# A mixture-of-experts kernel with six single tiles ahead of its paired units in place of seven, and its table of rows made in two single tiles

## The chip, the cores and the metric

The kernel runs on one core of a Trainium2 chip. Its time is the device time of one execution in microseconds (us); a profiled execution has in addition a span, from its first to its last instruction. TensorE (PE) multiplies matrices and transposes through a product with an identity; it writes to PSUM, of which the kernel holds eight banks PB[0] to PB[7]. VectorE (DVE) and ScalarE (ACT) read PSUM and do everything elementwise. GpSimd (POOL) issues the indirect transfers, which gather and scatter rows by a list of row numbers. SyncE (SP) issues the plain transfers. All engines run their own programs in order and wait for each other by semaphores.

## The reference

4096 tokens (64 x 64) of 256 values; every token goes to two of eight experts. An expert is a three-layer network 256 -> 512 -> 512 -> 256.

```python
var = jnp.mean(x * x, axis=-1, keepdims=True)
xn = rms_w * (x * jax.lax.rsqrt(var + EPS))
gate = xn @ wg_W + wg_b + (genre_embed @ gg_W + gg_b)
gate_w = jax.nn.softmax(gate, axis=-1)
topk_w, topk_i = jax.lax.top_k(gate_w, TOP_K)          # TOP_K = 2
cw = jnp.sum(jax.nn.one_hot(topk_i, E, dtype=x.dtype) * topk_w[..., None], axis=-2)
h1 = jax.nn.relu(jnp.einsum('bsh,ehm->bsem', x, W1) + b1)
h2 = jax.nn.relu(jnp.einsum('bsem,emn->bsen', h1, W2) + b2)
out_e = jnp.einsum('bsen,enh->bseh', h2, W3) + b3
out = x + jnp.einsum('bseh,bse->bsh', out_e, cw)
```

The reference computes every expert for every token and weights the result with `cw`, which is zero for six of the eight. The kernel computes only the two that count.

## The kernel before

The 8192 pairs of a token and an expert are put into tiles of 128 pairs of one expert. The routing is found in two parts: part A (`pA`) holds the first eight tokens of each partition, part B (`pB`) the other 24.

**Single tiles.** The first `F` = 7 tiles are one each of experts 0 to 6, filled with the first 128 pairs of that expert in part A. Their row numbers (`idxA`) are known early, so TensorE can work on them while the rest of the routing is computed. A single tile is gathered into `xg`, transposed (`transpose_x`), and goes through `layer1`, `layer2` and `layer3`: 8, 16 and 4 products, each of which the trace shows as two instructions. `head_step(u)` writes the program of single tile u: layer 1 of u, the transposes of tile u+1, layer 3 of u−1, layer 2 of u. The last single tile is done by `step`.

**The table of rows.** All pairs that are left are numbered by expert and tile; `idxR` is the list of their rows, one column per tile. It is made by products: for each of 64 pairs per partition (2 choices x 32 tokens) VectorE makes a one-hot of the place within a tile (`ohl`, from `lo16`) and one of the tile's number (`ohh`, a compare of `whole`, a row of tile numbers, with `hi16`), multiplies the latter with the token's number (`ohv`), and TensorE adds up 64 products in PB[7] (`table`, L646). VectorE does this in four chunks of 16 pairs (`rest`, L779 to L790), `idxR` follows from the sum in four operations (L794 to L797), and POOL gathers the rows of the first two units (`gather_unit`). `rest` is a generator, and `until(label)` writes its program up to a label; so `head_step` sets which piece stands where in the engines' programs.

**Units.** What is left is done in units of one expert: four tiles (512 columns), then one last unit for each expert, 9 to 16 strips of 32 columns wide, then pairs of tiles (256 columns). `SHAPES` lists combinations of (units of four, pairs, widths of the last units in falling order); the kernel has one program of the tail for each, and the first shape into which the counts fit is taken. A unit is wider than a tile and done by `step_fast` with the seven products of Strassen's method in Winograd's form (`Fast`): layer 1 of the unit is `f`, layer 2 is `g`; `f.p(k)` are its products, `f.mix(k)` differences of the inputs by VectorE, `f.fold` sums of weight blocks by VectorE, `f.c11` and so on the sums that form the blocks of the result, `f.r1`, `f.r22`, `f.r21` the relus by ScalarE. For the first unit (u == F) `transpose_x` turns its four gathered tiles (`xgE`) through TensorE into PB[4] and PB[7]; VectorE copies one half of the features into `xT` and ScalarE the other (L943). The rows of later units are turned through a scratch array and VectorE's transposes.

**Weights of the pairs.** `pB.weights` and `pB.spread` form each token's weight for each expert, three elementwise operations on POOL (L452 to L454), and write them to `cwdR`, from which `gather_cw` reads them by row.

The order in the program is written by hand; nothing is moved by a scheduler.

Of the kernel before, what the change touches and what calls it, by code (L numbers as in the profile page):

```python
# [12 lines left out]
F16 = mybir.dt.float16  # L13
# [8 lines left out]
SHAPES = [  # L22
# [26 lines left out]
]  # L49
# [3 lines left out]
def kernel(  # L53
# [17 lines left out]
    nc = tc.nc  # L71
# [18 lines left out]
    NPAIR = NT * TOPK  # L90
    F = E - 1

# [228 lines left out]
    class Part:  # L321
# [127 lines left out]

        def spread(self, cwd, cw8, i0):  # L450
            by_token = [self.ohe[:, k].rearrange("p e i -> p i e") for k in range(TOPK)]
            nc.gpsimd.tensor_tensor(self.cw8, by_token[0], self.over_e(self.t["den"]), ALU.mult)  # L452
            nc.gpsimd.tensor_tensor(self.w, by_token[1], self.over_e(self.t["d2"]), ALU.mult)
            nc.gpsimd.tensor_tensor(self.cw8, self.cw8, self.w, ALU.add)  # L454
            nc.gpsimd.dma_start(cwd.rearrange("(p i) e -> p i e", p=P)[:, i0 : i0 + cw8.shape[1], :], cw8)

# [182 lines left out]

    mms, placed = [], []  # L640

# [6 lines left out]
    def rest():  # L648
# [121 lines left out]
        LW, HW = P * GC // 2, NREST * GC // 2  # L770
        ohh = bigf[:, 0:HW].bitcast(F16).rearrange("p (g t) -> p g t", g=GC)

        def cols(c):
            return slice(c * GC, (c + 1) * GC)

        def low_of(c):
# [4 lines left out]

        ohls = [low_of(0)]
        for c in range(NCH):
            b0 = HW + (c % 3) * (LW + HW) + LW
            ohv = bigf[:, b0 : b0 + HW].bitcast(F16).rearrange("p (g t) -> p g t", g=GC)
            if c:
                ohls.append(low_of(c))
            V.tensor_tensor(ohh, whole, hi16[:, cols(c)].unsqueeze(2).to_broadcast([P, GC, NREST]), ALU.is_equal)
            i0 = c * GC % NI
            V.tensor_tensor(ohv, ohh, tokw[:, i0 : i0 + GC], ALU.mult)  # L790
# [3 lines left out]
        V.tensor_scalar(sa, tab, 0.0, -1.0, ALU.is_gt, ALU.mult)  # L794
        V.tensor_scalar(sb, tab, 0.0, float(NT), ALU.is_equal, ALU.mult)
# [129 lines left out]
    def transpose_x(u):  # L925
        bs, w, s0 = tiles(u), len(tiles(u)), slots(u).start
        if u > F:
            for k in range(w):
                V.transpose(  # L929
                    xT[:, :, s0 + k, :].rearrange("p c (b k) -> p k c b", b=SQ),  # L930
                    shs[:, s0 + k].rearrange("p k (a c) -> p k c a", a=SQ),
                )
            return
        if u < F:
            tps = [PB[4][:, c * BT : (c + 1) * BT] for c in range(HC)]
        else:
            tps = [PB[4], PB[7]]
        for c in range(HC):
            for k, b in enumerate(bs):
                g = ring(run, [P, H], "xg", 3, b) if u < F else xgR[(u - F) % 2][:, k]  # L940
                nc.tensor.transpose(tps[c][:, ts(k, BT)], g.rearrange("p (r c) -> p c r", c=HC)[:, c], ident)
            if u == F:
                (nc.scalar.copy if c else V.tensor_copy)(  # L943
                    xT[:, c, slots(u), :], tps[c].rearrange("p (s t) -> p s t", s=w)
                )
        if u < F:
            nc.scalar.copy(xT[:, :, s0, :], PB[4][:, 0 : HC * BT].rearrange("p (c t) -> p c t", c=HC))

# [125 lines left out]
    class Fast:  # L1074
# [108 lines left out]
        def c22(self):  # L1183
            V.tensor_tensor(self.dst(1, 1), self.tall(self.U), self.q[2], ALU.add)  # L1184

        def relu(self, n, out, src):
            nc.scalar.activation(out, src, AF.Relu, bias=ww[self.u][1][:, self.l, n : n + 1])  # L1187
# [194 lines left out]
    behind_fills = []  # L1382
    NF = 4

    def head_step(u):
# [3 lines left out]
        for k in range(3 * u, min(3 * u + 3, F)):  # L1389
            gather_cw(k)  # L1390
        layer1(u)
        if u == 0:
# [15 lines left out]
        if u > 1:  # L1408
            scaled(u - 1, "A")
        if u == F - 2:  # L1410
            until("chunk1")
            table(2 * GC)
        if u == 2:
            layer3_of(u - 1, range(HB))
            ranks_of_rest()
            layer3_of(u - 1, range(HB, MC))
            until("kinds")
        else:
            layer3(u - 1)
        if u - 1 + RING < F:  # L1420
# [3 lines left out]
        if u in (2, 4):  # L1424
            nc.sync.dma_start(b3_sb[:, u + 2 : u + 4], b3[u + 2 : u + 4].unsqueeze(0).to_broadcast([P, 2, H]))
        if u == F - 2:
            until("chunk2")
            table(3 * GC)
            until("chunk3")
            layer2(u, {2: table})  # L1430
            until("fetched")
            stream_3(F, mybir.EngineType.SP)
            fill(1)
            stream_1(F + 1, mybir.EngineType.SP)
            stow(F + 1)
            shuffle(F + 1)
            give(u - 2)
            give(u - 1, held=held)
            until("spread")
            return  # L1440
        if u == 2:
            layer2(u, {0: pB.exps})
        elif u == 3:
            until("places")
            layer2(u, {1: spread_map})
        else:
            layer2(u)
        if u == 1:
            scaled(0, "A")
        if u != F - 3:  # L1450
            give(u - 1)
        if u == 1:
            until("counts")
        if u == F - 3:
            until("chunk0")
            stream_1(F, mybir.EngineType.SP)
            fill(0)

    def fill(k):
# [13 lines left out]
    def step(u, last):  # L1473
# [5 lines left out]
        if u < last:  # L1479
            layer1(u)  # L1480
            if u >= F:
                streams(u, last)
            stage_2(u)
# [38 lines left out]
    def step_fast(u, last):  # L1522

        if u == F:
            transpose_x(u)
        far = fetches_of(u, last)
# [12 lines left out]
        if u == F:  # L1539
            scaled(u - 1, "A")  # L1540
            layer3_of(u - 1, range(HB))
            f.p(1)
            f.mix(1)
            f.p(5)
            f.mix(2)
            f.mix(3)
            f.p(2)
            f.c11()
            f.mix(4)
            f.p(6)  # L1550
            f.p(3)
            f.c12()
# [3 lines left out]
            f.r22()  # L1556
            layer3_of(u - 1, range(HB, MC))
            f.p(4)
            f.r21()
            g.mix(1)  # L1560
# [161 lines left out]
    with tc.manual_schedule():  # L1722
# [5 lines left out]
        gather(2)  # L1728
        pA.spread(cwdA, pA.cw8, 0)
        other = rest()  # L1730

# [61 lines left out]
```

## Time and profile before

| | |
|---|---|
| median of 3 runs | 448.32 us (448.28 to 450.24) |
| profiled execution | 448.61 us, span 446.9 us |
| PE, DVE, ACT, POOL busy | 98%, 83%, 54%, 63% of the span |
| seven single tiles and the table | up to 75.60 us |
| first unit's transposes to the second product of its layer 2 | 75.60 to 88.71 us |
| five units of four tiles, eight last units, six pairs | from there on |

The times in the timelines count from the span's start. An instruction's duration overlaps with the next one's on TensorE, so what a piece of TensorE's program costs is read from the distance between starts. In brackets stands how long an engine was idle before an instruction and what ended the wait. "L646" is line 646 of the kernel; a line may be that of a helper.

### The profile page before, as it was taken

How to read it: one execution, taken by the hardware profiler on the slowest of the kernel's cores; microseconds unless marked ns; L12 is line 12 of the kernel's file. 1: busy time of each engine (PE TensorE's matmuls, PEld its weight loads, DVE VectorE, ACT ScalarE, POOL GpSimd, SP SyncE). 2: the span in 40 equal slices, each digit the busy share in tenths (PEclk: the TensorE clock that was granted, in tenths of full speed). 3: DMA queues.
4: the chain of work that ended last, by engine and by line, in shares of the span. 5: the costliest groups of instructions: out<-in, count | busy, mean ns of one | idle time of the engine just before them, and what ended most of it. 6: DMA issues, size and time to landing. Idle time of an engine off the chain costs nothing. (4 is left out here: it accounts for less than half of the span.)

```text
span 446.9 us, 9223 instructions
## 1 busy us (share of the span) xinstructions
PE 438.7 (98%) x2941; PEld 408.6 (91%) x2941; DVE 369.5 (83%) x967; ACT 242.2 (54%) x572; POOL 279.8 (63%) x237
## 2 busy tenths in 40 slices
PE   9999998999999999999999999999999999999995
PEld 8699997889898999989899999999999889999994
DVE  6898957697979888897979797988877879889962
ACT  5855533547382746555564737474454465655561
POOL 7846316778788877575858483848857447764323
PEclk9999999999999999999999999999999999999999
DMA  8999999579568575455547363736756545766312
GB/s 310 331 352 393 369 364 354 142 229 216 175 126 200 118 162 150 120 120 150 120 126 150 85 150 70 172 92 145 164 149 137 143 117 130 186 169 168 72 15 50
DMA packets 75983, 78.11 MB, mean 175 GB/s; under 512 B 35471, under 2 KB 64114, under 8 KB 75796
## 3 DMA queue, kind: packets, MB, share of 16 engines
q1 hardware_dynamic: 49376, 42.51, 30.0%
q0 software_dynamic: 14912, 17.60, 22.8%
q10 hardware_dynamic: 11636, 17.32, 11.9%
q8 instruction: 25, 0.41, 0.4%
q14 instruction: 34, 0.28, 0.2%
HBM read 61.81 MB, written 20.25 MB: 184 GB/s over the span
## 5 line engine op out<-in xcount | busy, mean ns | idle before, releaser
L1349 POOL DMA_INDIRECT out_dram<-ys,idxR x60 | 97.9, 1632 | 88.6 <-DVE ys L1335 46.8
L1166 PE MATMUL pb<-hid,big 128*128 128x256 f32 (+7 forms) x456 | 84.6, 329 | 0.0
L1187 ACT ACTIVATE hid<-hid,bb 128x256 f32<-128x256 f32 (+12 forms) x152 | 73.1, 530 | 15.5 <-DVE hid L1184 6.3
L874 POOL DMA_INDIRECT cg<-cwdR,idxR x60 | 67.4, 1123 | 19.9 <-issue 17.7
L1166 PEld LDWEIGHTS pb<-hid,big 128*128 128x128 f32 x456 | 72.1, 191 | 4.9 <-issue 0.8
L1175 ACT COPY q1s<-pb 128x512 f32<-128x512 f32 (+7 forms) x57 | 27.5, 482 | 62.1 <-PE pb L1166 61.2
L1166 PE MATMUL pb<-mixB,big 128*128 128x256 f32 (+7 forms) x304 | 56.3, 328 | 0.0
L1175 ACT COPY big<-pb 128x512 f32<-128x512 f32 (+7 forms) x57 | 27.5, 482 | 52.1 <-PE pb L1166 52.1
L1166 PE MATMUL pb<-hotA,big 128*128 128x256 f32 (+7 forms) x304 | 53.2, 328 | 0.0
L1288 PE MATMUL pb<-w3r,hid 128*128 128x256 f32 (+1 forms) x216 | 51.2, 381 | 0.0
L1166 PEld LDWEIGHTS pb<-mixB,big 128*128 128x128 f32 x304 | 48.5, 191 | 2.8
L1166 PEld LDWEIGHTS pb<-hotA,big 128*128 128x128 f32 x304 | 47.9, 191 | 2.9
L1166 PE MATMUL pb<-mixX,iotx 128*128 128x256 f32 (+7 forms) x228 | 46.9, 328 | 0.0
L874 POOL DMA_INDIRECT xgE<-in_x_dram,idxR x32 | 35.8, 1119 | 17.6 <-DVE ib L802 8.2
L1288 PEld LDWEIGHTS pb<-w3r,hid 128*128 128x128 f32 (+1 forms) x216 | 39.1, 190 | 5.2 <-issue 0.8
L1166 PEld LDWEIGHTS pb<-mixX,iotx 128*128 128x128 f32 x228 | 37.4, 191 | 2.5 <-ACT q1s L1175 0.2
L874 POOL DMA_INDIRECT big<-in_x_dram,idxR x28 | 32.2, 1149 | 8.5 <-issue 7.9
L1187 ACT ACTIVATE hid<-pb,bb 128x256 f32<-128x256 f32 (+7 forms) x76 | 27.8, 417 | 15.3 <-PE pb L1166 12.6
L1166 PE MATMUL pb<-xT,w1r 128*128 128x256 f32 (+7 forms) x152 | 31.2, 328 | 0.0
L929 DVE STREAM_TRANSPOSE xT<-gTs 128x256 f32<-128x256 f32 x56 | 29.5, 632 | 0.0
L1067 PE MATMUL pb<-hid,w2a 128*128 128x128 f32 x224 | 27.1, 276 | 0.0
L1067 PEld LDWEIGHTS pb<-hid,w2a 128*128 128x128 f32 x224 | 26.4, 192 | 0.3
(342 smaller groups left out, 841.8 us busy)
## 6 DMA issues: line engine op xcount, KB each, us to landing
w3r<-in_L_cond_W_dram ACTq DMA_DIRECT2D x17, 512.0 KB, 4.7
w2a<-in_L_cond_W_dram SPq DMA_DIRECT2D x8, 1024.0 KB, 13.7
w1r<-in_L_cond_W_dram ACTq DMA_DIRECT2D x16, 512.0 KB
w1r<-in_L_cond_W_dram SPq DMA_DIRECT2D x10, 512.0 KB, 9.5
w3r<-in_L_cond_W_dram SPq DMA_DIRECT2D x9, 512.0 KB, 12.3
big<-in_x_dram SPq DMA_DIRECT2D x8, 512.0 KB, 5.4
gTs<-scr SPq DMA_DIRECT2D x8, 512.0 KB, 4.5
out_dram<-in_x_dram SPq DMA_DIRECT2D x4, 768.0 KB
```

Of the source, the lines that this page charges most:

```text
L874: return nc.gpsimd.indirect_dma_start(out=dst, out_offset=None, in_=src, in_offset=bass.IndirectOffsetOnAxis(ap=index(b), axis=0), bounds_ ...
L929: V.transpose(xT[:, :, s0 + k, :].rearrange("p c (b k) -> p k c b", b=SQ), shs[:, s0 + k].rearrange("p k (a c) -> p k c a", a=SQ),)
L1067: nc.tensor.matmul(ph, lhsT=w2[:, m, ts(n, P)], rhs=hid[0][:, m, 0:BT], start=(m == 0), stop=(m == MC - 1))
L1166: nc.tensor.matmul(bank[:, ts(n, self.w)], lhsT=w[:, c, ts(n, P)], rhs=x[:, c], start=new and n == 0 and c == 0, stop=n == HB - 1 and c == ...
L1175: nc.scalar.copy(self.q[(1, 6, 5).index(k)], self.tall(self.X if k == 5 else self.U))
L1187: nc.scalar.activation(out, src, AF.Relu, bias=ww[self.u][1][:, self.l, n : n + 1])
L1288: nc.tensor.matmul(sums(u, k)[0 : cols.stop - cols.start], lhsT=hid[1][:, n, cols], rhs=w3[:, n, :], start=(i == 0), stop=(i == MC - 1))
L1349: add = nc.gpsimd.indirect_dma_start(out=orows, out_offset=bass.IndirectOffsetOnAxis(ap=index(b)[0:n], axis=0), in_=y[0:n], in_offset=None ...
```

## The change

- `F` is 6: there is no single tile of expert 6; its rows go into the units. `idxR` has 71 columns, not 70, and `SHAPES` is a new list of 26.
- For chunks 1 to 3 ScalarE writes `hi16` out to the full size (`spread_high`), and VectorE's compare reads that in place of a spread-out operand. Two places (`homes`) hold it in turn.
- Chunks 0 and 1 and the first 32 table products now stand in `head_step(4)`, chunks 2 and 3, the weights, the other 32 products and `idxR` in `step(5)` (`rows_of_rest`), behind layer 1 of the last single tile.
- `pB.weights` and `pB.spread` stand ahead of the table's last operations; `spread` runs on VectorE, its write to `cwdR` on SP's queue.
- For the first unit the tiles are turned by twos: two tiles, copied, then `f.p(1)`, the third tile, `f.p(2)`, the fourth, copied. The order of products and differences is new. `p4_apart` puts product 4 into a bank of its own; ScalarE copies it and VectorE adds it (`c21`), and `r2` is the relu.

```diff
 SHAPES = [
-    (5, 6, (16, 15, 15, 14, 12, 11, 10, 9)),
...
+    (5, 6, (16, 16, 15, 15, 14, 11, 10, 9)),
...
-    F = E - 1
+    F = E - 2
...
-        ohls = [low_of(0)]
+        spread_high.append(lambda c: nc.scalar.copy(high_at(c), across(c)))
+        yield "spreads"
+        ohls = []
         for c in range(NCH):
...
-            V.tensor_tensor(ohh, whole, hi16[:, cols(c)].unsqueeze(2).to_broadcast([P, GC, NREST]), ALU.is_equal)
+            V.tensor_tensor(ohh, whole, ohh if c else across(c), ALU.is_equal)
...
+        pB.weights()
+        pB.spread(cwdR, cw8B, 0, V, nc.sync)
+        yield "spread"
         V.tensor_scalar(sa, tab, 0.0, -1.0, ALU.is_gt, ALU.mult)
...
-        pB.weights()
-        nc.gpsimd.tensor_copy(cw8B[:, 0:NA, :], pA.cw8)
-        pB.spread(cwdR, cw8B, 0)
-        yield "spread"
...
+        def p4_apart(self, bank):
+            a22, out = self.blocks()[2], bank[:, 0 : HB * self.w]
+            for n in range(HB):
+                for c in range(self.k):
+                    nc.tensor.matmul(
+                        out[:, ts(n, self.w)],
+                        lhsT=a22[:, c, ts(n, P)],
+                        rhs=self.t[3][:, c],
+                        start=n == 0 and c == 0,
+                        stop=n == HB - 1 and c == self.k - 1,
+                        skip_group_check=True,
+                    )
+            nc.scalar.copy(self.q[0], self.tall(out))
+        def c21(self):
+            V.tensor_tensor(self.dst(1, 0), self.tall(self.U), self.q[0], ALU.add)
...
+        elif u == 4:
+            until("chunk0")
+            table(GC)
+            spread_high[0](2)
+            until("chunk1")
+            layer2(u, {0: lambda: spread_high[0](3), 2: lambda: table(2 * GC)})
...
+    def rows_of_rest():
+        until("chunk3")
+        until("spread")
+        table()
+        until("fetched")
...
         if u == F:
-            transpose_x(u)
+            f = Fast(u, 0)
+            turn_tile(u, 0)
+            turn_tile(u, 1)
+            turned_two(u, 0)
+            scaled(u - 1, "A")
+            layer3_of(u - 1, range(HB))
+            f.p(1)
+            turn_tile(u, 2)
+            f.p(2)
+            f.c11()
+            turn_tile(u, 3)
+            turned_two(u, 2)
+            f.mix(1)
+            f.mix(2)
...
-            layer3_of(u - 1, range(HB, MC))
-            f.p(4)
-            f.r21()
+            f.p4_apart(PB[3])
+            f.c21()
+            f.r2()
             g.mix(1)
```

What this moves, at the two places of which the prediction speaks. A row is the line, the operation, what it writes and reads, and its size. First VectorE, at the end of the chunks (`big` holds the one-hots, `pb_75` is the bank of the table). Before:

```order
L788 TENSOR_TENSOR big<-whole,hi_575 128x1120
L790 TENSOR_TENSOR big<-big,xgE 128x1120
L794 TENSOR_SCALAR sa<-pb_75 128x70
L795 TENSOR_SCALAR sb<-pb_75 128x70
L796 SCALAR_TENSOR_TENSOR sa<-pb_75,sa 128x70
L797 TENSOR_TENSOR idxR<-sa,sb 128x70
```

After:

```order
L800 TENSOR_TENSOR big<-whole,big 128x1136
L802 TENSOR_TENSOR big<-big,xgE 128x1136
L446 TENSOR_REDUCE denB<-wB 128x24
L447 RECIPROCAL denB<-denB 128x24
L448 TENSOR_TENSOR d2B<-d2B,denB 128x24
L452 TENSOR_TENSOR cw8B<-ohB,denB 128x192
L453 TENSOR_TENSOR wB<-ohB,d2B 128x192
L454 TENSOR_TENSOR cw8B<-cw8B,wB 128x192
L809 TENSOR_SCALAR sa<-pb_75 128x71
```

The last compare reads `big`, where ScalarE has written, in place of `hi`; the weights and the three column operations stand between the last one-hot and the table's first operation.

Second TensorE, from the last product of layer 2 of the last single tile into the first unit (`pb0` to `pb7` are the banks, `xgE` the gathered rows, `hid1` with `w3r` is layer 3 of the single tile). Before:

```order
L1067 MATMUL pb3_71<-hid0_90,w2a_85 128x128 x4
L941 MATMUL pb4_72<-ident_92,xgE_186 128x128 x4
L941 MATMUL pb7_75<-ident_92,xgE_186 128x128 x4
L1295 MATMUL pb5_73<-w3r0_86,hid1_91 128x256 x2
L1166 MATMUL pb0_68<-xT_188,w1r1_83 128x256 x2
L1166 MATMUL pb1_69<-mixX_193,iotx_112 128x256 x2
```

After:

```order
L1080 MATMUL pb3_71<-hid0_90,w2a_85 128x128 x4
L953 MATMUL pb4_72<-ident_92,xgE_186 128x128
L953 MATMUL pb7_75<-ident_92,xgE_186 128x128
...
L1330 MATMUL pb6_74<-w3r2_88,hid1_91 128x256 x2
L1179 MATMUL pb0_68<-xT_188,w1r0_82 128x256 x2
...
L1179 MATMUL pb2_70<-xT_188,w1r0_82 128x256 x2
...
L1330 MATMUL pb6_74<-w3r2_88,hid1_91 128x256 x2
L1179 MATMUL pb1_69<-mixX_193,iotx_112 128x256 x2
```

Where eight transposes stood in a row ahead of everything, two tiles are turned ahead of the first half of layer 3 and `f.p(1)` (into `pb0`), one ahead of `f.p(2)` (into `pb2`) and one behind it; `f.p(5)` (into `pb1`), which needs a difference of the inputs, comes behind the second half of layer 3.

More of the change, by code (lines that the diff above doesn't have):

```diff
@@ L448, in weights, with spread @@
             V.tensor_tensor(d2, d2, den, ALU.mult)
-        def spread(self, cwd, cw8, i0):
+        def spread(self, cwd, cw8, i0, eng=nc.gpsimd, queue=nc.gpsimd):
             by_token = [self.ohe[:, k].rearrange("p e i -> p i e") for k in range(TOPK)]
[L452 to L455, printed above, removed]
+            eng.tensor_tensor(self.cw8, by_token[0], self.over_e(self.t["den"]), ALU.mult)
+            eng.tensor_tensor(self.w, by_token[1], self.over_e(self.t["d2"]), ALU.mult)
+            eng.tensor_tensor(self.cw8, self.cw8, self.w, ALU.add)
+            queue.dma_start(cwd.rearrange("(p i) e -> p i e", p=P)[:, i0 : i0 + cw8.shape[1], :], cw8)
     pA, pB = Part("A", 0, NA), Part("B", NA, NI)
@@ L638, in last_upright @@
         pB.norm(False)
-    mms, placed = [], []
+    mms, placed, spread_high = [], [], []
     def table(n=TOPK * NI):
@@ L770, in rest, with high_at, across @@
         LW, HW = P * GC // 2, NREST * GC // 2
-        ohh = bigf[:, 0:HW].bitcast(F16).rearrange("p (g t) -> p g t", g=GC)
+        homes = (0, HW + 3 * (LW + HW))
+        assert homes[1] + HW <= NG * TPB * H - GA * TPB * H
         def cols(c):
             return slice(c * GC, (c + 1) * GC)
+        def high_at(c):
+            h0 = homes[c % 2]
+            return bigf[:, h0 : h0 + HW].bitcast(F16).rearrange("p (g t) -> p g t", g=GC)
+        def across(c):
+            return hi16[:, cols(c)].unsqueeze(2).to_broadcast([P, GC, NREST])
         def low_of(c):
@@ L785, in rest @@
             ohv = bigf[:, b0 : b0 + HW].bitcast(F16).rearrange("p (g t) -> p g t", g=GC)
-            if c:
-                ohls.append(low_of(c))
-            V.tensor_tensor(ohh, whole, hi16[:, cols(c)].unsqueeze(2).to_broadcast([P, GC, NREST]), ALU.is_equal)
+            while len(ohls) <= min(c + (c > 0), NCH - 1):
+                ohls.append(low_of(len(ohls)))
+            ohh = high_at(c)
+            V.tensor_tensor(ohh, whole, ohh if c else across(c), ALU.is_equal)
             i0 = c * GC % NI
@@ L933, in transpose_x, with turn_tile, turned_two @@
             return
[L934 to L937, printed above, removed]
         for c in range(HC):
[L939 to L947, printed above, removed]
+            g = ring(run, [P, H], "xg", 3, u)
+            nc.tensor.transpose(PB[4][:, ts(c, BT)], g.rearrange("p (r c) -> p c r", c=HC)[:, c], ident)
+        nc.scalar.copy(xT[:, :, s0, :], PB[4][:, 0 : HC * BT].rearrange("p (c t) -> p c t", c=HC))
+    def turn_tile(u, k):
+        g = xgR[(u - F) % 2][:, k]
+        for c, bank in enumerate((PB[4], PB[7])):
+            nc.tensor.transpose(bank[:, ts(k, BT)], g.rearrange("p (r c) -> p c r", c=HC)[:, c], ident)
+    def turned_two(u, k0):
+        tps = [PB[4], PB[7]]
+        for c in range(HC):
+            (nc.scalar.copy if c else V.tensor_copy)(
+                xT[:, c, k0 : k0 + 2, :], tps[c][:, k0 * BT : (k0 + 2) * BT].rearrange("p (s t) -> p s t", s=2)
+            )
     def arena(t, sizes):
@@ L1184, in c22, with r2 @@
             V.tensor_tensor(self.dst(1, 1), self.tall(self.U), self.q[2], ALU.add)
+        def p4_apart(self, bank):
[9 more added lines that the diff above has]
+                        skip_group_check=True,
+                    )
+            nc.scalar.copy(self.q[0], self.tall(out))
+        def c21(self):
+            V.tensor_tensor(self.dst(1, 0), self.tall(self.U), self.q[0], ALU.add)
+        def r2(self):
+            for n in range(HB):
+                x = self.dst(1, 0)[:, n]
+                self.relu(HB + n, x, x)
         def relu(self, n, out, src):
@@ L1383 @@
     NF = 4
+    KNOWN = 5
     def head_step(u):
@@ L1391, in head_step @@
         layer1(u)
+        if u == 4:
+            spread_high[0](1)
         if u == 0:
@@ L1409, in head_step @@
             scaled(u - 1, "A")
-        if u == F - 2:
-            until("chunk1")
-            table(2 * GC)
         if u == 2:
-            layer3_of(u - 1, range(HB))
             ranks_of_rest()
-            layer3_of(u - 1, range(HB, MC))
             until("kinds")
-        else:
-            layer3(u - 1)
+        if u == KNOWN:
+            rows_of_rest()
+        layer3(u - 1)
         if u - 1 + RING < F:
@@ L1425, in head_step @@
             nc.sync.dma_start(b3_sb[:, u + 2 : u + 4], b3[u + 2 : u + 4].unsqueeze(0).to_broadcast([P, 2, H]))
[L1426 to L1440, printed above, removed]
         if u == 2:
@@ L1449, in head_step @@
             scaled(0, "A")
-        if u != F - 3:
+        if u < F - 3:
             give(u - 1)
@@ L1454, in head_step @@
         if u == F - 3:
-            until("chunk0")
             stream_1(F, mybir.EngineType.SP)
             fill(0)
+        if u == F - 2:
+            stream_3(F, mybir.EngineType.SP)
+            fill(1)
+            stream_1(F + 1, mybir.EngineType.SP)
+            give(u - 2)
+            give(u - 1, held=held)
+            if u == KNOWN:
+                stow(F + 1)
+                shuffle(F + 1)
+    def rows_of_rest():
[3 more added lines that the diff above has]
+        until("fetched")
     def fill(k):
@@ L1480, in step @@
             layer1(u)
+            if u == KNOWN:
+                rows_of_rest()
+                stow(F + 1)
+                shuffle(F + 1)
             if u >= F:
@@ L1539, in step_fast @@
         if u == F:
[L1540 to L1543, printed above, removed]
+            layer3_of(u - 1, range(HB, MC))
             f.p(5)
[L1545 to L1548, printed above, removed]
             f.mix(4)
             f.p(6)
+            f.mix(3)
             f.p(3)
@@ L1729 @@
         pA.spread(cwdA, pA.cw8, 0)
+        nc.gpsimd.tensor_copy(cw8B[:, 0:NA, :], pA.cw8)
         other = rest()
```

2 lines of the change are left out of this document (1 added, 1 removed), and 50 rows, old and new, of the table SHAPES.

## The prediction

> **What bounds the kernel.** I read the page first: the span, and how much of it each engine is busy.
> ```profile
> span 446.9 us, 9223 instructions
> PE 438.7 (98%) x2941; PEld 408.6 (91%) x2941; DVE 369.5 (83%) x967; ACT 242.2 (54%) x572; POOL 279.8 (63%) x237
> ```
> TensorE works 98% of the span, so an edit is worth what it takes from or adds to TensorE's program, plus what it does to the few waits. The list of waits for TensorE (engine, what it waited for, us in total, times, longest) names the largest:
> ```profile
> PE pb L941 <- DMA xgE<-in_x_dram,idxR: 1.6, 3, 0.9
> ```
> It is the first four-tile unit waiting for its gathered rows of x. The timeline of TensorE (start, us, line, output and inputs, count, and in brackets the idle time before) shows the stretch around it, and one ordinary single tile ahead of it:
> ```profile
> 49.74 1.95 PE L1057 MATMUL pb<-xT,w1r 128*128 128x128 f32 x16
> ...
> 51.76 1.89 PE L1288 MATMUL pb<-w3r,hid 128*128 128x256 f32 x8
> 53.49 3.73 PE L1067 MATMUL pb<-hid,w2a 128*128 128x128 f32 x32
> 57.06 1.95 PE L1057 MATMUL pb<-xT,w1r 128*128 128x128 f32 x16
> ...
> 59.08 2.12 PE L646 MATMUL pb<-big 128*128 128x70 f16 x32
> 61.04 1.97 PE L1288 MATMUL pb<-w3r,hid 128*128 128x256 f32 x8
> ...
> 72.03 3.73 PE L1067 MATMUL pb<-hid,w2a 128*128 128x128 f32 x32
> 75.60 0.28 PE L941 MATMUL pb<-ident,xgE 128*128 128x128 f32 x1
> 76.36 0.39 PE L941 MATMUL pb<-ident,xgE 128*128 128x128 f32 x1 [0.48 <-DMA xgE<-in_x_dram,idxR]
> ...
> 78.95 1.03 PE L1295 MATMUL pb<-w3r,hid 128*128 128x256 f32 x4
> 79.81 1.03 PE L1166 MATMUL pb<-xT,w1r 128*128 128x256 f32 x4
> ...
> 88.71 3.62 PE L1166 MATMUL pb<-hotA,big 128*128 128x256 f32 x16
> ```
> Ends are modelled, so I take distances between starts. A single tile costs 57.06 − 49.74 = 7.32 us. Layer 3 of one tile is 53.49 − 51.76 = 1.73, half the table of rows (32 products) is 61.04 − 59.08 = 1.96, layer 2 of a single tile 75.60 − 72.03 = 3.57. The unit after the single tiles begins its own products (p1) at 79.81, and at 88.71 TensorE issues the second product of its layer 2; from there no wait of note is left. I follow the change to that same product.
>
> **Part 1: one single tile fewer, −7.32 us of TensorE.** Its 128 rows don't vanish. Counting the two largest gates of every token of the reference's inputs, the expert that loses its single tile goes from 639 to 767 remaining rows, 20 to 24 strips of 32. The last unit of that expert widens from 12 to 16 strips, and the first shape of the new list fits. The starts of consecutive full units, and the products of the 12-strip unit (192 columns to a product):
> ```profile
> 168.77 1.03 PE L1166 MATMUL pb<-xT,w1r 128*128 128x256 f32 x4
> 193.15 1.03 PE L1166 MATMUL pb<-xT,w1r 128*128 128x256 f32 x4
> ...
> 301.99 2.76 PE L1166 MATMUL pb<-hotA,big 128*128 128x192 f32 x16
> 304.59 1.46 PE L1166 MATMUL pb<-hid,big 128*128 128x192 f32 x8
> ```
> A full unit costs 193.15 − 168.77 = 24.38 us. The 12-strip unit has 84 product instructions at 2.60 / 16 = 0.1625 us, 13.65, and three tiles of layer 3 at 1.73, 5.19: 18.84. **So the tail grows by 24.38 − 18.84 = 5.54 us**, and TensorE's whole work shrinks by only 1.78.
>
> **Part 2: when the rows of the first unit are known.** After the change the table's 64 products stand in the last two single tiles. TensorE, from the unchanged 49.74: 7.32 + 1.96 for tile 4 with half of the products, about 1.79 for layer 1 of tile 5 (51.76 − 49.74 = 2.02 holds two transposes besides), 1.96 for the other half ends at 62.77; layer 3 and layer 2, 1.73 + 3.57, end at 68.07. Before, the same point is 75.60: 7.53 sooner. VectorE must have the one-hots ready by 60.81. Its groups (mean ns of one before the bar's end) and its timeline:
> ```profile
> L788 DVE TENSOR_TENSOR big<-whole,hi 128x1120 f16<-128x1120 f16 x4 | 5.3, 1320 | 0.0
> L790 DVE TENSOR_TENSOR big<-big,xgE 128x1120 f16<-128x1120 f16 x4 | 3.0, 742 | 0.1
> L404 DVE TENSOR_TENSOR ohB<-gTs 128x192 f32<-128x192 f32 x2 | 1.2, 624 | 0.1
> L452 POOL TENSOR_TENSOR cw8B<-ohB,denB 128x192 f32<-128x192 f32 x1 | 1.2, 1243 | 0.0
> ```
> ```profile
> 60.25 1.23 DVE L779 TENSOR_TENSOR big<-iotx,lo 128x2048 f16<-128x2048 f16 x1 [1.39 <-PE pb L646]
> ...
> 62.75 0.74 DVE L790 TENSOR_TENSOR big<-big,xgE 128x1120 f16<-128x1120 f16 x1
> 67.74 0.23 DVE L794 TENSOR_SCALAR sa<-pb 128x70 f32<-128x70 f32 x1 [4.25 <-PE pb L646]
> ...
> 68.28 0.23 DVE L797 TENSOR_TENSOR idxR<-sa,sb 128x70 int32<-128x70 f32 x1
> ...
> 69.00 0.87 DVE L1335 SCALAR_TENSOR_TENSOR ys<-pb,cg,bc 128x256 f32<-128x256 f32 x2
> ...
> 70.60 0.35 DVE L1031 TENSOR_SCALAR bc<-b_sb,cg 128x256 f32<-128x256 f32 x1
> ...
> 76.49 0.68 DVE L1124 TENSOR_TENSOR big<-big 128x512 f32<-128x512 f32 x1
> ```
> The one-hots end at 63.49 with 1.39 of waiting inside. Three compares whose operand ScalarE has written out read packed data like L790; no row shows that compare, so it costs 0.74 to 1.32, and I take 0.74, the same size and type with no spread operand: 3 × 0.58 = 1.74 less. That gives 63.49 − 1.39 − 1.74 = 60.4, in time. (The two `give` steps of 0.4 that now stand between the chunks are about made up by the one taken from ahead of them and by the ranks, which now stand ahead of layer 3 of tile 1.) ScalarE's three copies are about 1.3 each, an estimate from the 0.59 that its 512 columns take at 80.88 below; they fall where it is half idle (54% on the page), and without that cover they would hold up their compares one for one. Then come the weight columns: the reductions, 70.60 − 69.00 − 0.80 = 0.8, and three operations that POOL did. They are bounded by L404 (0.62, strided as they are) and POOL's own 1.24; I take 0.62: the end is 60.4 + 0.8 + 1.9 = 63.1, against 64.9 at the upper bound. TensorE's last product ends at 62.77 and shows to VectorE at about 63.0. So TensorE and VectorE arrive together, and I put the first table operation at 63.1. POOL's timeline, and at the end a gather and the SP copy that waited for it:
> ```profile
> 68.78 1.04 POOL L874 DMA_INDIRECT xgE<-in_x_dram,idxR  x1 [8.18 <-DVE ib L802]
> 70.13 1.01 POOL L874 DMA_INDIRECT xgE<-in_x_dram,idxR  x1 [0.30 <-issue]
> ...
> 98.65 1.00 POOL L874 DMA_INDIRECT xgE<-in_x_dram,idxR  x1 [0.30 <-PE pb L1166]
> ```
> ```profile
> 101.45 0.38 SPq L913 DMA_DIRECT2D scr<-xgE  x1
> ```
> The first gather starts 68.78 − 67.74 = 1.04 after the first table operation, so at 64.1, **4.7 us sooner, while TensorE asks 7.53 sooner**. The second tile's gather starts 1.35 later and lands 76.36 − 70.13 = 6.23 after its start: 71.7. The gather at 98.65 landed within 2.8. What differs is the load on the DMA engines, by the windows (busy us of the engines, granted clock, and last the DMA share and GB/s):
> ```profile
> 57.06:75.60 18.54, 18.54 (x181) 18.08 (x179) 12.13 (x29) 6.55 (x18) 7.20 (x6) 1.00 1.05 389
> ```
> Weights and the filling of the output keep them full up to the first unit. The change drops two weight loads (1 MB, 2.6 us at 389 GB/s), so where they ran dry at about 76 they now do at 73 or later, and the rows of 64 to 72 still meet the load: I keep 6.23.
>
> [...] Here the loaded gather took 6.23 from start to landing and the unloaded one 2.8, so the trace sides with the load. [...]
>
> **Part 3: turning by twos.** TensorE is ready at 68.07, turns the first two tiles by 72.1, and does half of layer 3 (0.86) during the copy (about 0.42): p1 at 73.0. Before it was 79.81, so 6.8 sooner. From p1 to the product of 88.71 it took 8.90 before. After: seven products of 0.865, 6.05; half of layer 3, 0.86; two turns, 0.5; the first layer-2 product, 1.73: 9.14. Two new waits come on top. The second product waits for VectorE, which first does c11 (0.69), then the copy (0.42), then the first difference (0.43): about 0.4 uncovered. And the first difference of layer 2 now stands behind c21, which waits for ScalarE's copy of p4, queued behind four relus; by the durations of these (0.69, 0.59 and 2.13):
> ```profile
> 80.88 0.59 ACT L1175 COPY q1s<-pb 128x512 f32<-128x512 f32 x1 [0.74 <-PE pb L1166]
> ...
> 85.13 2.13 ACT L1187 ACTIVATE hid<-hid,bb 128x512 f32<-128x512 f32 x4 [1.07 <-DVE hid L1181]
> ```
> ```profile
> 79.39 0.43 DVE L1149 TENSOR_TENSOR mixX<-xT 128x256 f32<-128x256 f32 x1
> ...
> 82.67 0.69 DVE L1178 TENSOR_TENSOR hid<-pb,q1s 128x512 f32<-128x512 f32 x1 [1.99 <-PE pb L1166]
> ```
> the relus end 2.1 after c12, copy, c21 and difference follow, 0.59 + 0.69 + 0.69, while TensorE from p3's end has 1.73 of p7 and p4 and 1.73 of its first layer-2 product: 0.7 (c12) + 2.1 + 2.0 − 3.5, about 1.3 uncovered. The product of 88.71 comes at 73.0 + 9.14 + 1.7 = 83.8, **4.9 us sooner**.
>
> POOL loses the three column operations and the cwdR write. SP issues that write now; behind it in SP stand the loads for the second unit, which wait for that unit's gathers anyway, and the weights are read a unit later. The second unit's rows come 4.7 sooner too, against the 4.9 by which TensorE asks for them sooner. I cost these at nothing; if the 0.2 is exposed, that is their price.
>
> **The sum.** −4.9 + 5.54 = +0.6. The profiled execution took 448.61 (span 446.9, 1.7 around it): 449.2. The median of the runs is 0.3 lower, so **449.0 us**.
>
> **Rivals.**
> Early rows: if the rows land like the one at 98.65, the wait goes; but VectorE's sums of weight blocks end at 77.17, 8.89 after idxR began, less 1.6 for what has moved ahead (69.00 to 70.60), so at 70.9, and only then does it copy: p1 at 71.4, 1.6 sooner, **447.4**. For it: 1 MB less; against: the full window.
> VectorE last (slower): if the compare stays at 1.32 and the three column operations cost POOL's 1.24, VectorE ends at 60.4 + 1.74 + 0.8 + 3.7 = 66.6. It decides from 63.0 on: rows 3.5 later, **452.5**; with one of the two, 450.8. For it: no row shows either operation; against: L790 and L404.
> Cold TensorE (slower): the timeline's first rows show it.
> ```profile
> 0.86 3.75 PE L318 MATMUL pb<-const-float32-1.0 128*128 128x128 f32 x16 [0.86 <-PEq L1779]
> ```
> There 16 products took as long as the 32 at 72.03: half speed. If the new wait, 68.07 to 72.1 with only transposes in it, brings that back for 3.5 us, 1.75 is lost: **450.8**. Against: before, 75.60 to 78.95 held only transposes as well, and 78.95 to 79.81 ran four products at full speed. [...]
> The change not doing what it says: another shape taken in the tail. The counts speak against it.
>
> **Chances.** Forecast 0.62, early rows 0.15, VectorE last 0.13, cold 0.06, other 0.04. Half a per cent, 2.2 us, is about what a measurement can tell from no change: 446.1 to 450.6. Faster than that 0.06 (early rows and the sum of part 3 too dear by 1.3), slower 0.17, same 0.77. The range takes in early rows below and one late VectorE operation above: 446.9 to 451.0.
>
> **What would show it.** In the profile after: the compare near 0.75; the first gather of the unit near 64, p1 near 73.0, the second layer-2 product near 83.8, and two more waits on VectorE there; a unit more of 24.38. Wrong if p1 comes before 71 or after 75, or if the tail's growth is not 5.5.

## The result, and the profile after

The changed kernel took 453.33 us in the median of four runs (452.76 to 454.47), the kernel before 448.3 on the same chip: a ratio of 1.011 with a 95% interval of 1.0093 to 1.0127. It is slower by 1.1%, and above the range that the prediction gave. On the chips of the runs whose names begin with e, g and h, all engines show waits of 1 to 4 us without a cause in the program, in the kernel before as well (461 to 464 us), and the ratios there, taken over the executions within 1.5% of each kernel's fastest, lie 0.5 to 1.4% below those of the same kernels on the chips of f and i, so no time or ratio of theirs decides anything below and only stretches of their traces free of such waits are used.

The page's head and its engine row, and the list of TensorE's waits (engine, what it waited for, us in total, times, longest) of the kernel after:

```profile
span 451.0 us, 9185 instructions
...
PE 438.9 (97%) x2915; PEld 406.3 (90%) x2915; DVE 375.7 (83%) x983; ACT 246.3 (55%) x574; POOL 277.4 (62%) x233
```
```profile
PE pb L953 <- DMA xgE<-in_x_dram,idxR: 2.6, 1, 2.6
PE pb L1179 <- DVE hotA L1162: 1.1, 1, 1.1
...
PE pb L953 <- DMA w1r<-in_L_cond_W_dram: 0.6, 1, 0.6
PE pb L1179 <- DVE mixX L1162: 0.5, 1, 0.5
```

TensorE executes 26 instructions fewer, and its busy time is no less: 438.9 us against 438.7. The 1.6 us of waiting for rows have become 3.2 (the second piece, put down to a weight load, stands ahead of the second tile's turn and ends, as the same wait in f0 and f2 shows, when its rows are there), and the two waits for VectorE are new. TensorE's timeline from the wait to the product that the prediction followed (start, us, line; in brackets the idle time before):

```profile
71.02 0.47 PE L953 MATMUL pb<-ident,xgE 128*128 128x128 f32 x2 [2.58 <-DMA xgE<-in_x_dram,idxR]
72.10 0.50 PE L953 MATMUL pb<-ident,xgE 128*128 128x128 f32 x2 [0.60 <-DMA w1r<-in_L_cond_W_dram]
72.44 1.24 PE L1330 MATMUL pb<-w3r,hid 128*128 128x256 f32 x4
73.47 1.91 PE L1179 MATMUL pb<-xT,w1r 128*128 128x256 f32 x4
75.17 0.63 PE L953 MATMUL pb<-ident,xgE 128*128 128x128 f32 x2
75.60 1.49 PE L1179 MATMUL pb<-xT,w1r 128*128 128x256 f32 x4
...
78.74 1.99 PE L1179 MATMUL pb<-mixX,iotx 128*128 128x256 f32 x8 [0.55 <-DVE mixX L1162]
...
83.28 2.17 PE L1179 MATMUL pb<-hid,big 128*128 128x256 f32 x8
86.53 3.72 PE L1179 MATMUL pb<-hotA,big 128*128 128x256 f32 x16 [1.07 <-DVE hotA L1162]
```

p1 starts at 73.47 and the next instruction 1.70 us later; a product of this size took 0.865 before. The windows (busy us of PE, PEld, DVE, ACT, POOL, then the granted clock, the DMA share and GB/s) say why:

```profile
72.00:74.00 2.00, 1.90 (x8) 1.65 (x9) 0.94 (x2) 0.78 (x2) 1.56 (x2) 0.78 0.77 293
74.00:76.00 2.00, 2.00 (x7) 1.57 (x6) 0.00 (x0) 0.58 (x1) 0.74 (x1) 0.50 0.66 197
76.00:78.00 2.00, 2.00 (x10) 1.57 (x8) 0.80 (x2) 0.38 (x2) 0.96 (x1) 0.87 0.04 12
```

From what the clock lacks to 1 in these windows, it is at one half for (0.22 + 0.50 + 0.13) x 2 / 0.5 = 3.4 us, from about 1 us after the second tile's turn began. In the kernel before it is 1.00 in each of these windows.

The starts of units further on show the rest. First the kernel after, then before:

```profile
93.55 1.02 PE L1179 MATMUL pb<-xT,w1r 128*128 128x256 f32 x4
118.17 1.03 PE L1179 MATMUL pb<-xT,w1r 128*128 128x256 f32 x4
...
329.04 0.71 PE L1179 MATMUL pb<-xT,w1r 128*128 128x160 f32 x4
```
```profile
95.62 1.03 PE L1166 MATMUL pb<-xT,w1r 128*128 128x256 f32 x4
120.00 1.03 PE L1166 MATMUL pb<-xT,w1r 128*128 128x256 f32 x4
...
325.11 0.71 PE L1166 MATMUL pb<-xT,w1r 128*128 128x160 f32 x4
```

The last row of each is the seventh of the eight last units, behind the one that is wider. At the second unit the changed kernel is 2.07 ahead, at the third 1.83, and it keeps that until the last units, where it falls from 1.83 ahead to 3.93 behind: the wider unit costs 5.76 us.

### The profile page after: what moved, and what is told of

The parts are those of the page before. It is cut to its first block, busy times and chain, and to the rows that moved or that the text cites. A ratio compares the mean times of both kernels' runs of the same rounds, so it can differ in the third digit from the quotient of the medians.

```text
span 451.0 us, 9185 instructions
## 1 busy us (share of the span) xinstructions
PE 438.9 (97%) x2915; PEld 406.3 (90%) x2915; DVE 375.7 (83%) x983; ACT 246.3 (55%) x574; POOL 277.4 (62%) x233
## 5 line engine op out<-in xcount | busy, mean ns | idle before, releaser
L1179 PE MATMUL pb<-hid,big 128*128 128x256 f32 (+6 forms) x456 | 86.2, 332 | 0.0
L1222 ACT ACTIVATE hid<-hid,bb 128x256 f32<-128x256 f32 (+11 forms) x154 | 74.7, 534 | 17.2 <-DVE hid L1197 6.6
L1188 ACT COPY q1s<-pb 128x512 f32<-128x512 f32 (+6 forms) x57 | 27.8, 487 | 64.1 <-PE pb L1179 59.8
L1179 PE MATMUL pb<-mixB,big 128*128 128x256 f32 (+6 forms) x304 | 57.1, 331 | 0.0
L1188 ACT COPY big<-pb 128x512 f32<-128x512 f32 (+6 forms) x57 | 27.8, 487 | 51.3 <-PE pb L1179 50.2
L1179 PE MATMUL pb<-hotA,big 128*128 128x256 f32 (+6 forms) x304 | 54.1, 331 | 1.1 <-DVE hotA L1162 1.1
L1179 PE MATMUL pb<-mixX,iotx 128*128 128x256 f32 (+6 forms) x228 | 47.5, 332 | 0.5 <-DVE mixX L1162 0.5
L1222 ACT ACTIVATE hid<-pb,bb 128x256 f32<-128x256 f32 (+6 forms) x74 | 27.1, 417 | 15.8 <-PE pb L1179 14.6
L1179 PE MATMUL pb<-xT,w1r 128*128 128x256 f32 (+6 forms) x152 | 33.0, 341 | 0.0
L1179 PEld LDWEIGHTS pb<-xT,w1r 128*128 128x128 f32 x152 | 26.2, 198 | 2.0
```

The costliest lines, as they stand in the source:

```text
L1179: nc.tensor.matmul(bank[:, ts(n, self.w)], lhsT=w[:, c, ts(n, P)], rhs=x[:, c], start=new and n == 0 and c == 0, stop=n == HB - 1 and c == ...
L1188: nc.scalar.copy(self.q[(1, 6, 5).index(k)], self.tall(self.X if k == 5 else self.U))
```

## Experiments

All times are medians in us; the first letter of a name stands for the chip, and the ratio is to the kernel before on the same chip, with its 95% interval.

| run | what | before | time | ratio |
|---|---|---|---|---|
| f0_after | the changed kernel | 448.48 | 453.37 | 1.0102 (1.0085 to 1.0120) |
| e1_busy, f1_busy | TensorE kept busy in the wait | 462.17, 448.48 | 462.48, 451.01 | 0.9966 (0.9917 to 1.0016), 1.0055 (1.0036 to 1.0074) |
| e3_fills, f2_fills | two fills later | 462.17, 448.48 | 459.41, 451.04 | 0.9899 (0.9858 to 0.9941), 1.0042 (1.0026 to 1.0058) |
| g2_both | both of these | 463.97 | 462.39 | 0.9959 (0.9922 to 0.9996) |
| e4_p4 | fourth product as before | 462.17 | 462.55 | 1.0009 (0.9966 to 1.0051) |
| e2_seven, f3_seven | seven single tiles | 462.17, 448.48 | 462.59, 449.71 | 0.9933 (0.9885 to 0.9981), 1.0024 (1.0006 to 1.0042) |
| g3_order, h2_order | and the old order of products | 463.97, 461.2 | 463.59, 458.32 | 0.9976 (0.9940 to 1.0012), 0.9932 (0.9903 to 0.9961) |
| g1, h1, i1_best | and two fills later | 463.97, 461.2, 448.8 | 461.24, 457.78, 446.39 | 0.9864 (0.9817 to 0.9912), 0.9873 (0.9832 to 0.9913), 0.9950 (0.9932 to 0.9969) |
| g4, h3, i2_prefill | before with two fills later | 463.97, 461.2, 448.8 | 464.04, 461.37, 450.38 | 0.9981 (0.9954 to 1.0008), 0.9983 (0.9949 to 1.0017), 1.0030 (1.0013 to 1.0048) |

### Is the half clock a cost, and does the wait cause it?

```diff
+            keep(12)      # products of constants, 128x128
             turn_tile(u, 0)
+            keep(3)
             turn_tile(u, 1)
```

> The changed kernel with 15 products of constants (128x128, into an unused part of a bank) put on TensorE where it only waits for the first two tiles of the first four-tile unit: 12 ahead of the first tile's turn, 3 ahead of the second's. They are extra work and take nothing away. Theory (the wait lets TensorE's clock drop): granted clock 1.00 from 68 to 78 us, p1 0.87 long instead of 1.70, the product after it on the path about 1.7 us sooner, 451.6 us in place of 453.3, and the four executions closer together. Rival (the clock drops for another reason, or the lost 1.7 us are waits that only look like it): 453.3 us or a little more, p1 still at 1.70.

> The changed kernel itself, beside the three variants of it, since the first four ran on a chip where the kernel before took 462 us with waits of 1 to 2.6 us strewn over TensorE for which the profile has no releaser, and the changed kernel wasn't among them. Both theories expect 1.011 of before on a quiet chip: clock at half from 73 to 77 us.

> The 15 products of constants in TensorE's wait once more. Theory (cold clock): 1.4 to 1.7 us below the changed kernel of the same call, as p1 took 0.97 and not 1.70 and p1 to the second layer-2 product 11.6 us and not 13.06 in the first trace of it. Rival (waits that only look like it): level with the changed kernel.

In e1's trace the clock is at 1.00 through this stretch. f0 and f1 ran on one chip. The changed kernel came out as the first time, 453.37, and f1 at 451.01, 2.36 us lower although TensorE does more. Its six executions have a granted clock of 0.998 to 1.000 over the whole span; the changed kernel's lie at 0.989 to 0.996. The windows of f1's profiled execution:

```profile
72.00:74.00 2.00, 1.14 (x6) 0.69 (x5) 1.97 (x5) 0.78 (x2) 1.50 (x2) 1.00 0.88 324
74.00:76.00 2.00, 1.09 (x6) 0.99 (x7) 0.86 (x2) 0.00 (x0) 1.29 (x1) 1.00 0.43 153
```

The clock stays at 1.00, so it is the wait that lets it drop. One spell of 3.4 us at half clock can cost at most half of it, 1.7; why f1 gained 2.36 the trace doesn't tell, as its profiled execution (452.48) was the slowest of the six, and its second layer-2 product comes at 86.53, no sooner than in the changed kernel's first trace. It shows what is next behind the wait: there p1 waited for VectorE's copy of the turned rows, which stood behind the sums of weight blocks, and these had waited 3.51 us for a weight load.

```profile
74.91 1.13 PE L1185 MATMUL pb<-xT,w1r 128*128 128x256 f32 x4 [1.77 <-DVE xT L964]
```

### Are the rows late because the DMA engines are full?

The fills copy x to the output, ahead of the tokens' results.

```diff
             stream_1(F, mybir.EngineType.SP)
-            fill(0)
...
             stream_3(F, mybir.EngineType.SP)
-            fill(1)
...
+            fill(0)
+            fill(1)
             fill(2)
```

> The changed kernel with the first two of the four copies that fill the output moved from tiles 3 and 4 to behind the last single tile, beside the third. Theory (the rows are late because the DMA engines are full): the second tile of rows lands 1 to 2.5 us sooner than 72.1, TensorE's wait falls under 3 us, the clock stays up, p1 comes near 72 and takes 0.87: 450 to 451 us in place of 453.3. Rival (a gather's time does not hang on the load): rows at 72.1 as before and 453.3; or the later copies collide with the second unit's rows: 454 or more, with a new wait at the second unit.

> The first two fills of the output behind the last single tile once more. Theory (late rows from full DMA engines): p1 near 72.2 and the second layer-2 product near 83.7, 2.85 us ahead of the changed kernel's 86.53, so 450.5 us where the changed kernel takes 453.3. Rival (the three fills now standing together hold up the second unit): part of this is given back at 92 to 110 us and the time is 452 or more.

TensorE's timeline of f2_fills:

```profile
70.17 0.47 PE L953 MATMUL pb<-ident,xgE 128*128 128x128 f32 x2 [1.58 <-DMA xgE<-in_x_dram,idxR]
71.39 0.55 PE L953 MATMUL pb<-ident,xgE 128*128 128x128 f32 x2 [0.74 <-DMA xgE<-in_x_dram,idxR]
71.73 1.92 PE L1330 MATMUL pb<-w3r,hid 128*128 128x256 f32 x4
73.44 1.87 PE L1179 MATMUL pb<-xT,w1r 128*128 128x256 f32 x4
```

In f0, on the same chip, the two tiles were turned at 71.89 and 72.84, so the rows came 1.5 to 1.7 us sooner, as the theory has it; against the changed kernel's first trace (71.02 and 72.10) it is 0.7 to 0.9. The busy share of the DMA engines from 68 to 72 was 0.60 in f2 (0.83 and 0.36 in its halves) and 1.03 in f0. But in this execution the clock dropped again (layer 3's half took 1.71, p1 1.70). In e3, whose trace has no foreign wait up to 83 us, it did not: one wait of 1.81, and then products at full speed.

```profile
70.53 0.94 PE L953 MATMUL pb<-ident,xgE 128*128 128x128 f32 x4 [1.81 <-DMA xgE<-in_x_dram,idxR]
71.31 1.03 PE L1330 MATMUL pb<-w3r,hid 128*128 128x256 f32 x4
72.17 1.03 PE L1179 MATMUL pb<-xT,w1r 128*128 128x256 f32 x4
```

f2's twelve executions fall into two groups, five from 449.02 to 449.74 and seven from 450.88 to 451.84, whose means are 2.0 apart; the granted clock over the span is 0.998 in the mean of the first and 0.995 in that of the second, to which the profiled one belongs. So with the wait this short the drop seems to come in some executions and not in others. That isn't shown, as only one of the twelve has a trace, and f1's six lie in two groups too (450.77 to 451.01 and 452.46 to 452.48) with a clock of 0.998 or more in both. The expected 450.5 lies between them. The lower group is 3.9 below the changed kernel and still 1.0 above before.

> The changed kernel with both mendings: the products of constants in the wait and the first two fills later. Theory (cold clock and late rows are two separate costs): p1 near 72.6 with a clock of 1.00 in every execution, the second layer-2 product near 84.1, 449.5 us without the two groups 2 us apart that the later fills alone left; still not under before, as the wider unit of the tail costs 5.75 and the new order 2.6. Rival (both mend the same 2.3 us): 451.0 as with either of them.

g2's ratio of 0.9959 can't be set against f1's and f2's, so whether both add up was not settled by it. In its trace p1 took 0.87 and the clock was up.

### The order of the first unit's products

> The changed kernel with the fourth product of the first unit as it was before the change: into the common bank, relu straight from it, the second half of the single tile's layer 3 ahead of it instead of ahead of the fifth product. Theory (the first difference of the unit's layer 2 is held up by the sum behind ScalarE's copy): TensorE's wait of 1.07 us at the second layer-2 product goes, the wait for the first difference of x ahead of the fifth product grows from 0.55 to 1.4: 452.3 to 453.1 us, so little moves. Rival (the sum is what the path hangs on alone): 451.8 us.

```diff
-            layer3_of(u - 1, range(HB, MC))
             f.p(5)
...
-            f.p4_apart(PB[3])
-            f.c21()
-            f.r2()
+            layer3_of(u - 1, range(HB, MC))
+            f.p(4)
+            f.r21()
```

```profile
79.76 1.99 PE L1179 MATMUL pb<-mixX,iotx 128*128 128x256 f32 x8 [1.41 <-DVE xT L958]
...
87.04 3.62 PE L1179 MATMUL pb<-hotA,big 128*128 128x256 f32 x16
```

As expected, one wait went (1.07 to none at the product) and the other grew (0.55 to 1.41). From p1 (74.49) to the product are 12.55 in place of 13.06. The two can be compared because the clock dropped at the same point of both, 0.34 and 0.35 us ahead of p1 (at 73.13 and 74.14); in f0, where it dropped sooner, the same stretch took 12.04. The gain is half a microsecond, too little for the times on that chip to show.

Seven single tiles with all the rest of the change, which needs only `F = E - 1` and the old `SHAPES`:

> The changed kernel with seven single tiles and the old list of shapes; everything else of the change stays (known rows in tile 5, ScalarE's write-out, weight columns on VectorE, the turn by twos). Theory: the rows are asked for at 64 us and TensorE asks for them only near 75.5, so there is no wait for rows and no cold clock; the second layer-2 product of the first unit comes 11.4 us after p1, and p1 near 76.7: about 0.6 us sooner than before, 447.7 us, and the tail's 5.8 us are gone. Rival (removing the single tile was worth its 7.3 us in itself, and what costs is elsewhere in the change, such as the new order of the first unit's products): 449 us or more, slower than before although nothing waits for rows.

> Seven single tiles and the old shapes with all the rest of the change, once more. Theory: no wait for rows, clock 1.00, p1 near 76.7, p1 to the second layer-2 product 11.5 us, so 88.2 against 88.71 before: 447.8 us. Rival: in the first trace TensorE waited 2.4 us there for VectorE's copy of the turned rows, since VectorE's sums of weight blocks stood behind a weight load until 85; if that is the load on the DMA engines and not that chip, p1 comes at 79 or later and the time is 450 us or more.

f3's time is 449.71, not the 447.8 of the theory. The single tile alone makes 453.37 − 449.71 = 3.7 us of the loss; but with it back the change still doesn't pay. TensorE's and VectorE's timelines of f3_seven:

```profile
79.48 1.13 PE L1179 MATMUL pb<-xT,w1r 128*128 128x256 f32 x4 [2.25 <-DVE xT L958]
...
91.16 3.72 PE L1179 MATMUL pb<-hotA,big 128*128 128x256 f32 x16 [1.09 <-DVE hotA L1162]
```
```profile
73.55 0.43 DVE L1131 TENSOR_TENSOR iotx<-w1r 128x256 f32<-128x256 f32 x1 [7.15 <-DMA w1r<-in_L_cond_W_dram]
...
79.01 0.42 DVE L958 COPY xT<-pb 128x256 f32<-128x256 f32 x1
```

The rows are there, and p1 comes hardly sooner than before (79.81), because VectorE's sums wait for the unit's weights until 73.55: the rival of that expectation held (in e2's trace the same wait is 2.40). And from p1 to the product are 11.68 us at a full clock, where the kernel before took 8.90. To see whether the order makes that difference, the first unit was turned whole and its products put back, with the early table kept:

```diff
-            turn_tile(u, 0)
...
+            turned_four(u)
...
+            f.p(1)
+            f.mix(1)
+            f.p(5)
+            f.mix(2)
...
+            layer3_of(u - 1, range(HB, MC))
+            f.p(4)
+            f.r21()
```

> As g1_best, with the fills where they were. Theory: VectorE waits for the first unit's weights until 73.5 as in f3_seven, its sums end at 79.0, p1 comes near 79.8, the same as before, and the old order keeps 8.9 us to the second layer-2 product: 448.4 us, no change from before although the rows are known 4 us sooner, and 1.3 less than f3_seven (449.7). Rival (the order of the products isn't what f3_seven lost): 449.7 us.

> g3_order once more, for the same reason. Theory (the new order of the products is what f3_seven lost to before): p1 near 79.8 as there, 8.9 us to the second layer-2 product, 448.4 us, 1.3 below f3_seven's 449.7. Rival (the early table itself slows something else): 449.7 us.

The expected times can't be judged on these chips, but in h2's trace the stretch itself has no foreign wait:

```profile
82.15 1.03 PE L1188 MATMUL pb<-xT,w1r 128*128 128x256 f32 x4
...
91.05 3.62 PE L1188 MATMUL pb<-hotA,big 128*128 128x256 f32 x16
```

8.90 us, as before to the hundredth. So the new order makes this stretch 11.68 − 8.90 = 2.8 us longer. Two of the turns, 0.22 and 0.23 in f3, stood ahead of p1 in the old order, so about 2.3 of it are lost.

### What is left of the change when its costs are taken away

Seven single tiles, the old order, and the two fills later:

> Seven single tiles and the old shapes, the first unit turned whole and its products in their old order, the first two fills behind the last single tile; the early table, ScalarE's write-out and the weight columns on VectorE stay. Theory (what costs is the new order of the first unit's products, 11.6 us from p1 to the second layer-2 product against 8.90 before, and VectorE's sums of weight blocks behind late weights): TensorE has no wait for rows, p1 near 77.3, the product near 86.2, 2.5 us sooner than before: 446 us, faster than both kernels. Rival (the weights of the first unit land no sooner without the fills): VectorE's sums still end near 79, p1 at 79.8 and 448.4 us.

> g1_best once more, as its chip strewed waits of 1 to 3.6 us over TensorE and VectorE for which the profile has no releaser. There VectorE's sums of weight blocks ended at 79.2 less the 2.7 us that it waited for TensorE, and all rows had landed when TensorE turned them. Theory as there: p1 near 77.3, the second layer-2 product 8.9 us later, 446 us. Rival (the new order isn't the cost, or the weights of the first unit land too late): 448.4 us or more.

> g1_best a third time, for its time on a quiet chip. On two disturbed ones it took 0.986 and 0.987 of before, with a wait of 1.7 to 1.9 us of TensorE for VectorE's copy of the turned rows, which started 3.7 to 4.7 us after it could. Theory (old order, no late rows, no late weights): without that disturbance p1 near 77.3, the second layer-2 product near 86.2, 446 us. Rival (that wait belongs to the kernel): p1 at 79 or later, 448 us.

i1 has 446.39 against 448.8, ratio 0.995 (0.9932 to 0.9969), faster than the kernel before, and with it than the changed one. The time, p1 and the product come as the theory had them (446, 77.3, 86.2). TensorE and VectorE:

```profile
75.57 1.12 PE L966 MATMUL pb<-ident,xgE 128*128 128x128 f32 x8
77.39 1.03 PE L1188 MATMUL pb<-xT,w1r 128*128 128x256 f32 x4
...
86.29 3.62 PE L1188 MATMUL pb<-hotA,big 128*128 128x256 f32 x16
```
```profile
70.00 0.42 DVE L1140 TENSOR_TENSOR iotx<-w1r 128x256 f32<-128x256 f32 x1 [3.64 <-DMA w1r<-in_L_cond_W_dram]
...
76.24 0.69 DVE L967 COPY xT<-pb 128x512 f32<-128x512 f32 x1 [0.69 <-PE pb L966]
```

No bracket stands on TensorE's rows: all eight turns go in one piece, the weights land 3.55 sooner than in f3, and VectorE now waits for TensorE. The product comes 2.42 sooner than before, and the time is 2.41 lower.

Are the later fills all of it? The kernel before with nothing but these:

> The kernel before with nothing changed but its first two fills, which go behind the last single tile. Theory (the load on the DMA engines sets when rows and weights land there): the wait for rows at 75.6 to 78.95 shrinks by 1 to 2 us, 446.5 to 447.5 us. Rival (the early table is needed for that gain): 448.4 us, unchanged.

> g4_prefill once more, for the same reason. In its disturbed trace all four tiles of rows had landed at 76.8, where the kernel before waited for them until 78.25. Theory (the load on the DMA engines sets when rows land): TensorE's wait for rows goes, p1 then waits for VectorE's sums of weight blocks and comes near 78.5: 447.1 us. Rival: 448.4 us, unchanged.

> g4_prefill a third time, beside it. On the disturbed chips its rows had landed in time, but VectorE's copy came 4 us late. Theory (later fills alone mend the late rows of the kernel before; the early table adds what VectorE's sums then end sooner): p1 near 78.5, 447.1 us. Rival: that wait belongs to the kernel, and it stays at 448.4.

```profile
86.90 3.62 PE L1166 MATMUL pb<-hotA,big 128*128 128x256 f32 x16
...
98.76 1.99 PE L1166 MATMUL pb<-mixB,big 128*128 128x256 f32 x8 [1.34 <-DVE hid L1184]
```
```profile
97.64 0.44 DVE L1016 COPY cw<-cg 128x1 f32 x2 [1.92 <-DMA cg<-cwdR,idxR]
```

The product comes 1.8 sooner there too, and then more than that is given back: VectorE waits for the gathered weight columns (0.98 and 1.92 us), TensorE for VectorE. The time is 450.38, slower than before, against both the theory (447.1) and the rival (448.4). In i1, where the columns are made on VectorE ahead of the table's end and written by SP, that wait doesn't appear. So the later fills pay only with the rest of the change; whether it is the early columns that they need, or the early table, no run separates. The other way round, f3 shows that with the fills in their place the first unit's weights come too late for the early rows to be of use.

## Why the prediction was wrong, step by step

**Part 1, the single tile, held.** The tail grew by 5.76, 5.54 was predicted. That the swap of a narrow for a wide unit leaves 1.6 of the 7.32 us was read rightly.

**Part 2, when the rows are known, held.** The rows on VectorE and POOL after:

```profile
58.49 0.74 DVE L800 TENSOR_TENSOR big<-whole,big 128x1136 f16<-128x1136 f16 x1
...
60.76 0.62 DVE L452 TENSOR_TENSOR cw8B<-ohB,denB 128x192 f32<-128x192 f32 x1
...
63.10 0.23 DVE L809 TENSOR_SCALAR sa<-pb 128x71 f32<-128x71 f32 x1 [0.81 <-PE pb L646]
```
```profile
64.15 1.07 POOL L885 DMA_INDIRECT xgE<-in_x_dram,idxR  x1 [5.58 <-DVE ib L817]
```

The compare with its operand written out takes 0.74 (predicted 0.74), the first column operation 0.62 (0.62), the table's first operation starts at 63.10 (63.1), the first gather at 64.15 (64.1). VectorE was 0.8 sooner than summed and waited 0.81 for the last products, which set the start. The second tile is turned at 72.10 (71.7 predicted). The rival "VectorE last" fell with the first two rows, "early rows" with the 72.10.

**Part 3, turning by twos, is where it failed**, and there in two of its terms. It put p1 at 73.0 and the followed product 10.84 later, at 83.8, 4.9 sooner than before. p1 came at 73.47, and the product 13.06 later, at 86.53: 2.18 sooner.
- *The clock.* The wait for rows was foreseen at the right place and length, and the half clock was priced rightly among the rivals (1.75; the windows allow 1.7). But "Cold TensorE" was given a chance of 0.06, because the 3.35 us in which the kernel before did hardly more than transpose had not tripped it. That comparison was the error: of those 3.35 us TensorE was idle for 0.48 + 0.23 + 0.88 = 1.6, and here for 3.2 of 4.0; what the runs show of such idle times stands in the last section. From p1 to the second half of layer 3, 3.69 us passed here and 2.29 in f3: 1.4 of the 1.7 lie there, another 0.17 in the half of layer 3 ahead of p1.
- *The order.* Without these 1.4 p1 to product is 11.66 (11.68 in f3), not 10.84: of the 2.8 that the order adds to 8.90, the sum had 1.9. The two waits were foreseen well, 0.4 and 1.3 against 0.55 and 1.07; but the products around them were added up at 0.865 each, as if TensorE ran on. Next to the waits they took longer: the layer 3 ahead of the first takes 1.03 and not 0.86, layer 2's first eight instructions 2.17 and not 1.73, and p1 in f3, behind its wait, 0.97.

The remainder is small: the second unit took 24.62 where before had 24.38, it started 0.11 later behind the followed product, and the last stretch lost 0.2. Added up: 0.47 (p1) + 1.4 + 0.82 + 0.24 + 0.11 + 0.22 (the tail) + 0.2 = 3.5, and that is what the span's growth, 4.1, has over the prediction's sum, 0.64. The median lies 0.6 above the profiled execution.

**What the sum hid.** The forecast was near zero because −4.9 and +5.54 nearly cancelled, and so every error of Part 3 showed whole. The swap of the tile looked free in TensorE's work, but took away the 7 us under which gather, weights and sums had been landing.

## What to carry to other kernels

Work that an engine does while data lands is cover: before it is removed, add up what lands under it and when, since TensorE doesn't only wait for the rest but may come out of the wait at half its clock, as it did here for 3.4 us. Judge such a wait by how long TensorE is idle within it, not by how long nothing but transposes runs: in this case 1.6 us (before) and 1.81 (e3) brought no drop, 3.2 (after), 3.6 (e4) and 3.9 (f0) did, and in between f2's 2.32 did while f3's 2.25 and e2's 2.40 did not. An order of products that starts sooner but waits twice is costed with what the products ahead of each wait lose, here 0.17 and 0.44 us.

## What the runs showed of the hardware

At this place the half clock lasted 3.4 us in each of four profiled executions (after, f0, f2, e4), though TensorE's two waits there came to 3.2, 3.9, 2.3 and 3.6 us. The 1.6 us of the kernel before, in three waits, brought no drop, nor did the 1.81 of e3 in one. In between the length alone doesn't tell the cases apart: f2's 2.32, in two waits (1.58 and 0.74), brought a drop, while behind f3's 2.25 and e2's 2.40, each in one wait, the clock is at 1.00 (in f3 from 66 to 100 us, in e2 from 86 to 100). What decides between these was not shown.

A gather started by POOL landed later here while the DMA engines were full: with two of the fills moved away, rows asked for at about the same time (64.3 in f2, 64.1 in f0) came 1.5 to 1.7 us sooner in f2 than in f0, and 0.7 to 0.9 sooner than in the changed kernel's first trace; the engines' busy share from 68 to 72 was 0.60 in f2 and 1.03 in f0 and in that trace.
